# Expert weights copied three tiles ahead, and a dense item placed last: a change to the end of a vision tower kernel

## The chip, the cores and the metric

The kernel runs on one core of one Trainium2 chip. The metric is the device time of the whole kernel in microseconds, lower is better. The core has five engines that work side by side and wait for one another through semaphores: PE (TensorE, matmuls), DVE (VectorE), ACT (ScalarE), POOL (GpSimd, which here issues the indirect DMAs and a few powers) and SP (SyncE, which issues most other DMAs). Sixteen DMA engines move the data.

## The reference

The input is cut into patches and embedded (32 blocks of 512 tokens, 256 features each), run through one retention layer with an MLP, and then through a mixture of 8 experts of which each token uses two:

```python
logits = tokens @ router_w.T
probs = softmax(logits)
rw, re = top_k(probs, 2)
rw = rw / rw.sum(-1)
combine = zeros((N, E)).at[arange(N)[:, None], re].set(rw)
out = tokens
for e in range(8):
    h = gelu(tokens @ w1[e] + b1[e])
    y = h @ w2[e] + b2[e]
    out = out + combine[:, e:e+1] * y
```

Here `tokens` are the layer-normed outputs of the layer before, and the final result is those outputs plus `out`. All matmuls are in float32.

## The kernel before

A block of 512 tokens goes through embedding, retention, MLP and the router. Block 0 to 30 then *scatter* each token's row twice, once for each of its two experts, to a buffer in DRAM (`xbuf`) that has a region for each expert (`place`, eight indirect DMAs on GpSimd for a block). `take` looks how many *tiles* of 256 rows of one expert are full, and puts them into the list of tiles. A tile is worked through in stages, all driven by `expert_step`: `load` fetches its rows and its expert's weights, `turn` makes xT of the rows, `enter` multiplies by the first matrix, `leave` by the second, and adds the 256 results to `out` with two scatter-adds.

```python
    def expert_step():
        n = at["enter"]
        advance("load", n + AHEAD)       # AHEAD = 4
        advance("turn", n + 2)
        advance("fetch", n + 3)
        advance("enter", n + 1)
        advance("leave", n)
```

`advance(what, upto)` runs the stage `what` for all tiles before number `upto` that have not had it. PE, DVE, ACT and SP execute their instructions in the order in which this program emits them; the order on POOL is chosen by a scheduler.

Most tiles get their weights by a DMA in `load`. For the last 22 tiles (4 that are taken with block 29's choice, 18 with block 30's) all eight experts' weights are loaded once into SBUF, into `bank`, and VectorE copies the right one into the tile's buffer `w`:

```python
    def load_bank():
        ...
        for e in range(E):
            nc.scalar.dma_start(out=bank[0][:, e, :], in_=wex[ts(e, P), :])
            ...

        def fetch(self):                              # class Tile
            if self.block.i >= NS - 2:
                e = nc.vector.value_load(self.table[:, 2, t : t + 1], ...)
                nc.vector.tensor_copy(self.w.unsqueeze(1), bank[0][:, bass.ds(e, 1), :])
```

As the expert's number is only known at run time, such a copy waits for the whole bank. The end of `leave` scatters the sums; two pairs of scatter-adds may hit the same row, so a pair waits for the pair before it:

```python
            y = four.tile([P, 2, D], F32, name="y")
            nc.vector.tensor_tensor(y, ps, ..., ALU.add)               # L765
            for c in range(2):
                nc.vector.tensor_scalar(y[:, c, :], ...)               # L767
            before = added[-2:] + [self.block.stored]
            for c in range(2):
                add = nc.gpsimd.indirect_dma_start(out=out, ..., in_=y[:, c, :],
                                                   compute_op=ALU.add) # L771
                unordered("sums", add, before)
                added.append(add)
```

The last block (31) is not scattered. Its tokens go through all eight experts as *dense items* (`Expert(e, last)`), which stand in the same list as the tiles: an `enter` of eight matmuls (L803), a `leave` of sixteen (L820), and a sum into `h` on VectorE, weighted by the token's share. The last one stores `h`.

The stretch behind the main loop, where everything changed lies (NS is 31):

```python
        last, mid, old = blocks[NS], blocks[NS - 1], blocks[NS - 2]
        ...                                   # bank loads are issued in between
        old.choose()
        expert_step()
        next(weights)
        mid.mlp_out(0)
        next(weights)
        take(NS - 1, old, old.place())
        expert_step()
        mid.mlp_out(1)
        last.retention(0)
        mid.features3()
        mid.rows()
        last.retention(1)
        for t in range(TT):
            mid.logits(t)
        mid.choose()
        expert_step()
        writes = mid.place()
        last.residual()
        expert_step()
        expert_step()
        expert_step()
        mid.pads(writes)
        take(NS, mid, writes)

        last.features2()
        for m in range(KH):
            last.mlp_in(m)
        expert_step()
        last.mlp_out(0)
        expert_step()
        last.mlp_out(1)

        rest = tiles[at["load"] :]
        del tiles[at["load"] :]
        for e in range(E):
            tiles.extend(rest[len(rest) * e // E : len(rest) * (e + 1) // E])
            tiles.append(Expert(e, last))
        expert_step()
        expert_step()
        last.features3()
        ...                                   # logits of the last block
        last.choose()
        last.combine()
        while at["leave"] < len(tiles):
            expert_step()
```

Of the kernel before, what the change touches and what calls it, by code (L numbers as in the profile page):

```python
# [30 lines left out]
def vit_tower_kernel(  # L31
# [20 lines left out]
    E = rw.shape[1]  # L52
# [35 lines left out]
    def load_x(i):  # L88
        xb = xpool.tile([P, XW], F32, name="xb")
        nc.sync.dma_start(out=xb, in_=x[i // NBLK, i % NBLK])  # L90
        return xb
# [91 lines left out]
    def fold(w, g, b, to):  # L183

        n, M = w.shape[1], w.shape[3] // P
        ps = p_sm.tile([P, n * M], F32, name="sm")
        for i in range(n):
            for m in range(M):
                for k in range(KD):
                    nc.tensor.matmul(  # L190
                        ps[:, i * M + m : i * M + m + 1],
                        lhsT=w[:, i, k, ts(m, P)],
                        rhs=vec[:, b + k : b + k + 1],
                        start=k == 0,
                        stop=k == KD - 1,
                    )
        nc.vector.tensor_tensor(vec[:, to : to + n * M], vec[:, to : to + n * M], ps, ALU.add)
        for k in range(KD):
            nc.scalar.mul(w[:, :, k, :], w[:, :, k, :], vec[:, g + k : g + k + 1])
# [477 lines left out]
    def load_bank():  # L677

        early.close()
        late = ctx.enter_context(tc.tile_pool(name="late", bufs=1, side="right"))  # L680
        bank.append(late.tile([P, E, NW], F32, name="bank"))
        for e in range(E):
            nc.scalar.dma_start(out=bank[0][:, e, :], in_=wex[ts(e, P), :])
            loaded.append(e)
            yield

    AHEAD = 4
    tiles = []
# [155 lines left out]
    def advance(what, upto):  # L844
        while at[what] < min(upto, len(tiles)):
            getattr(tiles[at[what]], what)()
            at[what] += 1

    def expert_step():

        n = at["enter"]
        advance("load", n + AHEAD)
        advance("turn", n + 2)
        advance("fetch", n + 3)
        advance("enter", n + 1)
        advance("leave", n)

# [6 lines left out]
    def slot(known):  # L864

        if len(tiles) - at["enter"] > LEFT and at["enter"] + 2 <= known:
            expert_step()
# [7 lines left out]
    with tc.manual_schedule(engines=MANUAL):  # L875
        xs[1] = load_x(1)
        blocks[0].differences(xs.pop(0))
        for i in range(NS):
            new = blocks[i]
            known = len(tiles)  # L880
            mid = blocks[i - 1] if i >= 1 else None
            old = blocks[i - 2] if i >= 2 else None
            embed = new.embed()
            next(embed)
            if at["enter"] == 0:
                advance("turn", 2)
            if mid:
                mid.features2()
            if old:
                old.rows()  # L890
                old.turn3()
            next(embed)
            next(embed, None)
            slot(known)
            if old:
                old.join3()
            if i == 0:
                fold(wqkv_sb, G1, B1, BQ)
            for m in range(KH):
                if mid:  # L900
                    mid.mlp_in(m)
                if m == 1 and i:
                    new.split1()
                if m == TT - 1:
                    slot(known)
                if m == KH - 3:
                    new.features1()
            if old:
                for t in range(TT):
                    old.logits(t)  # L910
            blocks[i + 1].differences(xs.pop(i + 1))
            for m in range(KD):
                new.retention(m)
                if old and m == 0:
                    old.choose()
            if old:
                take(old.i + 1, old, old.place())
            if i + 2 < NB:
                xs[i + 2] = load_x(i + 2)
            slot(known)  # L920
            if mid:
                mid.mlp_out(0)
            new.residual()
            slot(known)
            if at["enter"] == 0:

                advance("load", 2)
            if i == 0:
                fold(w1_sb.unsqueeze(1), G2, B2, MB1)
            else:  # L930
                new.split2()
            if mid:
                mid.mlp_out(1)

        last, mid, old = blocks[NS], blocks[NS - 1], blocks[NS - 2]
        embed = last.embed()
        next(embed)
        mid.features2()
        old.rows()
        old.turn3()  # L940
        next(embed)
        next(embed, None)
        expert_step()
        weights = load_bank()
        old.join3()
        for m in range(KH):
            mid.mlp_in(m)
            if m in (1, 2, 4, 5, 7):
                next(weights)
            if m == 1:  # L950
                last.split1()
            if m == TT - 1:
                expert_step()
            if m == KH - 3:
                last.features1()
        for t in range(TT):
            old.logits(t)
# [4 lines that stand above are left out]
        mid.mlp_out(0)  # L962
        next(weights)
        take(NS - 1, old, old.place())
        expert_step()
        mid.mlp_out(1)
        last.retention(0)
        mid.features3()
# [22 lines that stand above are left out]
        rest = tiles[at["load"] :]  # L991
        del tiles[at["load"] :]
        for e in range(E):
            tiles.extend(rest[len(rest) * e // E : len(rest) * (e + 1) // E])
            tiles.append(Expert(e, last))
        expert_step()
        expert_step()
        last.features3()
        for t in range(TT):
            last.logits(t)  # L1000
# [4 lines that stand above are left out]
# [82 lines left out]
```

## Time and profile before

| what | value |
|---|---|
| time, median of three | 2275.05 us (2271.82 to 2275.25) |
| span of the profiled execution | 2277.5 us |
| PE busy | 2191.8 us, 96% |
| VectorE busy | 1490.3 us, 65% |
| GpSimd busy | 863.2 us, 38% |
| ScalarE busy | 784.9 us, 34% |
| scatter-adds to `out` (L771) | 262, 1655 ns each on GpSimd |
| copies of expert weights (L721) | 22, 0.83 us each |

A row of a timeline gives the start, the duration, the engine, the source line, the operation with the tile that it writes and those that it reads, and how many instructions were merged; the square bracket at the end says how long the engine was idle before it and which instruction released it. The releaser is inferred: an instruction that waits for several things is put down to the one that came last by the profile, and where the engine named had long been done it was another, often a DMA. The row of the page that shows PE's busy share in 40 slices of the span (56.9 us each) has it at nine tenths or more from the second slice on, except in the 37th (2050 to 2107 us) and in the last.

### The profile page before, as it was taken

Reading aid. Unit: us, or ns where it says so; the run is one execution under the profiler, and the core shown is the slowest. Engines: PE = TensorE matmul, PEld = TensorE weight load, DVE = VectorE, ACT = ScalarE, POOL = GpSimd, SP = SyncE. Lnnn points to the kernel's source line nnn. Section 1 sums busy time; section 2 is a strip of 40 time slices with the busy share of each in tenths; the row PEclk is TensorE's granted clock in tenths of the full one; section 3 lists DMA queues with packets and bytes.
Section 4 is the critical chain, followed back from the end, with each engine's and each line's share of the span. In section 5 each row is a group of like instructions: output and inputs, shape, how many; then the busy total and the mean of one; then the engine's idle time right before and its main releaser. Section 6 shows DMA issues by size and latency. Waiting matters only on the chain.

```text
span 2277.5 us, 28306 instructions
## 1 busy us (share of the span) xinstructions
PE 2191.8 (96%) x8652; PEld 1574.0 (69%) x8652; DVE 1490.3 (65%) x4427; ACT 784.9 (34%) x1213; POOL 863.2 (38%) x822
## 2 busy tenths in 40 slices
PE   3999999999999999999999999999999999997997
PEld 2666667777776677777667777676677777675775
DVE  6567666666666667666766666666667666757464
ACT  1222243333334333333343333334333333332332
POOL 0012224444443344443334444443444443335344
PEclk9999999999999999999999999999999999998999
DMA  5133357656656675566667656656665565595653
GB/s 150 28 94 82 102 128 158 136 128 135 143 129 131 150 158 118 130 140 138 136 131 159 132 130 134 143 128 132 152 152 123 131 140 137 117 180 111 120 68 46
DMA packets 461671, 289.14 MB, mean 127 GB/s; under 512 B 377936, under 2 KB 432336, under 8 KB 457424
## 3 DMA queue, kind: packets, MB, share of 16 engines
q1 hardware_dynamic: 410464, 214.44, 40.1%
q0 software_dynamic: 49632, 67.39, 16.9%
q10 hardware_dynamic: 1424, 5.52, 0.9%
q8 instruction: 68, 1.11, 0.2%
q14 instruction: 83, 0.68, 0.1%
HBM read 116.81 MB, written 88.39 MB: 90 GB/s over the span
## 4 chain that ended last, share of the span: by engine, by line
PE 51%; DVE 24%; POOL 11%; issue 7%; DMA 6%; ACT 0%; POOLq 0%; DVEq 0%; SPq 0%; ACTq 0%
PE mm L284 24%; PE tm L328 9%; POOL xbuf L576 8%; PE mm L734 5%; PE tm L751 5%; DMA out<-y,xg 4%; DVE ks L382 3%; DVE ret L392 3%; POOL out L771 2%; PE sm L493 2%; DVE kv L374 2%; DVE zz L238 2%; PE tm L442 2%; DVE h L417 1%; DVE h L416 1%
## 5 line engine op out<-in xcount | busy, mean ns | idle before, releaser
L771 POOL DMA_INDIRECT out<-y,xg x262 | 433.7, 1655 | 550.0 <-DVE y L767 302.4
L442 PE MATMUL tm<-w_sb,aT 128*128 128x256 f32 x2048 | 453.3, 379 | 1.7 <-DVE taken L671 1.1
L284 PE MATMUL mm<-hT,w_sb 128*128 128x512 f32 x1024 | 449.9, 593 | 1.6 <-ACT hT L278 1.1
L442 PEld LDWEIGHTS tm<-w_sb,aT 128*128 128x128 f32 x2048 | 388.6, 190 | 55.6 <-DVE taken L671 1.4
L284 PEld LDWEIGHTS mm<-hT,w_sb 128*128 128x128 f32 x1024 | 194.1, 190 | 223.0 <-issue 212.4
L284 PE MATMUL mm<-hT,wqkv_sb 128*128 128x512 f32 x768 | 342.9, 603 | 3.7 <-DVE hT L278 3.7
L576 POOL DMA_INDIRECT xbuf<-row,to x248 | 244.2, 985 | 257.2 <-DVE full L635 169.8
L742 ACT ACTIVATE ge<-mm,w 128x256 f32<-128x256 f32 x262 | 109.3, 469 | 522.0 <-issue 503.1
L284 PEld LDWEIGHTS mm<-hT,wqkv_sb 128*128 128x128 f32 x768 | 145.7, 193 | 175.8 <-issue 166.0
L734 PE MATMUL mm<-xT,w 128*128 128x256 f32 x1048 | 253.3, 385 | 9.7 <-DVE tile_share L760 9.1
L751 PE MATMUL tm<-w,ge 128*128 128x256 f32 x1048 | 248.8, 380 | 0.0
L434 ACT ACTIVATE aT<-mm,vec 128x512 f32<-128x512 f32 x256 | 171.3, 685 | 219.2 <-PE mm L284 218.2
L328 PE MATMUL tm<-weff,xd 128*128 128x256 f32 x1024 | 230.6, 384 | 16.8 <-DVE y L765 8.6
L328 PEld LDWEIGHTS tm<-weff,xd 128*128 128x128 f32 x1024 | 193.3, 191 | 53.2 <-DVE y L765 19.1
L734 PEld LDWEIGHTS mm<-xT,w 128*128 128x128 f32 x1048 | 196.2, 192 | 47.3 <-issue 23.2
L751 PEld LDWEIGHTS tm<-w,ge 128*128 128x128 f32 x1048 | 200.3, 191 | 31.1 <-issue 3.8
L727 ACT COPY xT<-xh 128x512 uint16<-128x512 uint16 x262 | 181.3, 761 | 39.7 <-DMA xh<-xbuf 32.4
L264 ACT COPY planes<-zz 128x1024 uint16<-128x1024 uint16 x122 | 121.5, 1043 | 206.0 <-DVE zz L238 206.0
L229 POOL TENSOR_SCALAR rstd<-mv 128x4 f32<-128x4 f32 x93 | 37.2, 400 | 328.2 <-DVE mv L210 326.1
L317 PE MATMUL tm<-wsum,xb 128*128 128x256 f32 x512 | 120.2, 389 | 25.8 <-ACT wsum L121 25.8
L238 DVE TENSOR_SCALAR zz<-z,mv,rstd 128x256 f32<-128x256 f32 x128 | 44.4, 410 | 137.7 <-POOL rstd L234 137.7
L533 POOL TENSOR_TENSOR ex<-euler,second 128x4 f32<-128x4 f32 x32 | 34.8, 1089 | 262.0 <-DVE second L525 262.0
(147 smaller groups left out, 2343.8 us busy)
## 6 DMA issues: line engine op xcount, KB each, us to landing
w<-in_wex SPq DMA_DIRECT2D x109, 641.5 KB
xb<-in_x SPq DMA_DIRECT2D x32, 1040.0 KB
out<-h SPq DMA_DIRECT2D x31, 512.0 KB
bank<-in_wex ACTq DMA_DIRECT2D x8, 641.5 KB
out<-y,xg POOLq DMA_INDIRECT x262
xbuf<-row,to POOLq DMA_INDIRECT x248
xh<-xbuf SPq DMA_TRANSPOSE x131
xg<-xbuf SPq DMA_DIRECT2D x131, 4.0 KB
```

Source lines behind the costliest of these rows:

```text
L264: nc.scalar.copy(planes[:, :, i * D : (i + 1) * D], half)
L284: nc.tensor.matmul(ps, lhsT=w[:, k, ts(m, P)], rhs=rhs[:, k, :], start=k == 0, stop=k == KD - 1)
L317: nc.tensor.matmul(ps[:, u, :], lhsT=od[:, j, ts(u, P)], rhs=wsum[:, j, :], start=j == 0, stop=j == J - 1)
L328: nc.tensor.matmul(ps[:, i, :], lhsT=xd[:, i, j, ts(u, P)], rhs=weff[:, i * J + j, :], start=j == 0, stop=j == J - 1,)
L434: nc.scalar.activation(self.aT[:, m, :], ps, AF.Relu, bias=vec[:, MB1 + m : MB1 + m + 1])
L442: nc.tensor.matmul(ps[:, i, :], lhsT=self.aT[:, k, ts(u * 2 + i, P)], rhs=w2_sb[:, k, :], start=k == 0, stop=k == KH - 1,)
L576: write = nc.gpsimd.indirect_dma_start(out=xbuf, out_offset=bass.IndirectOffsetOnAxis(ap=to[:, c, t : t + 1], axis=0), in_=self.row[:, t, ...
L727: nc.scalar.copy(halves[:, :, :, 1 - i], self.xh[:, i * KD : (i + 1) * KD, :])
L734: nc.tensor.matmul(ps[:, m, :], lhsT=self.w[:, k * D + m * P : k * D + (m + 1) * P], rhs=self.xT[:, k, :], start=k == 0, stop=k == KD - 1,)
L742: nc.scalar.activation(self.ge[:, m, :], ps[:, m, :], AF.Gelu, bias=self.w[:, 5 * D + m : 5 * D + m + 1])
L751: nc.tensor.matmul(ps[:, c, :], lhsT=self.ge[:, k, ts(c, P)], rhs=w[:, (2 + k) * D : (3 + k) * D], start=k == 0, stop=k == KD - 1,)
L771: add = nc.gpsimd.indirect_dma_start(out=out, out_offset=bass.IndirectOffsetOnAxis(ap=self.xg[:, c, NUMBER - D : NUMBER - D + 1], axis=0), ...
```

## The change

There are two edits, both behind the main loop. The first moves the copies of weights: a tile's copy is made as soon as its buffer is allotted in `load`, three tiles ahead of the one that enters and not two, and in the step behind block 29's `take` no copy is made at all, so that VectorE reaches no copy before it has worked through block 30's choice of experts. The three copies that have come due by then are made in the next step. It is meant to keep VectorE from standing still for the bank in front of work that others wait for, and PE from waiting for a copy. The second spreads the remaining tiles over the first seven dense items instead of over all eight, so that two dense items close the list and the last tile's sums are added while the last dense items still run.

```diff
-    def expert_step():
+    def expert_step(fetch=True):
 
         n = at["enter"]
         advance("load", n + AHEAD)
         advance("turn", n + 2)
-        advance("fetch", n + 3)
+        if fetch:
+            advance("fetch", n + AHEAD)
         advance("enter", n + 1)
         advance("leave", n)
 ...
         take(NS - 1, old, old.place())
-        expert_step()
+        expert_step(fetch=False)
         mid.mlp_out(1)
 ...
         for e in range(E):
-            tiles.extend(rest[len(rest) * e // E : len(rest) * (e + 1) // E])
+            tiles.extend(rest[len(rest) * e // (E - 1) : len(rest) * (e + 1) // (E - 1)])
             tiles.append(Expert(e, last))
```

In the built kernels the instructions of SP and their order are the same before and after, and so are those of POOL; PE, DVE and ACT have the same instructions in another order.

## The prediction, made before the changed kernel ran

> **What bounds the kernel now.** I read the page first: PE busy 96% of the span, so only what happens between matmuls can be gained. Every edit lies behind the main loop, so I then read the chain of waits from 2040 us on. I call the expert steps behind `take(NS - 1, ...)` A (where `fetch=False` is put), S1 (behind block 30's `choose`), S2, S3, S4 (behind `last.residual()`), S5 and S6 (in the last block's second half), S7 (behind `last.mlp_out(1)`'s matmuls, its y behind that item's VectorE work), S8 and so on.
>
> ```profile
> 2042.52 17.11 DMA bank<-in_wex
> 2059.75 0.83 DVE w L721
> ...
> 2067.86 2.33 PE mm L251 x8
> ...
> 2098.09 0.82 DVE w L721
> 2099.06 3.75 PE mm L734 x8
> ...
> 2262.50 4.18 DMA out<-y,xg
> 2266.80 0.71 issue
> 2267.51 1.54 POOL out L771
> ```
>
> Columns: start, duration, what. Twice a copy of an expert's weights (L721) stands ahead of PE on the path, the first behind the load of the bank. The end is not PE but GpSimd's scatter-adds. The timelines of PE, ScalarE and GpSimd give the sizes:
>
> ```profile
> 2054.51 5.31 PE L284 MATMUL mm<-hT,wqkv_sb 128*128 128x512 f32 x12
> 2067.86 2.33 PE L251 MATMUL mm<-ident,tok 128*128 128x128 f32 x8 [8.04 <-DVE rstd L223]
> ...
> 2084.16 1.99 PE L734 MATMUL mm<-xT,w 128*128 128x256 f32 x8 [0.64 <-ACT xT L727]
> ...
> 2099.06 3.75 PE L734 MATMUL mm<-xT,w 128*128 128x256 f32 x8 [7.73 <-DVE tile_share L760]
> ```
>
> ```profile
> 2082.72 1.39 ACT L727 COPY xT<-xh 128x512 uint16<-128x512 uint16 x2 [8.42 <-DMA xh<-xbuf]
> ```
>
> ```profile
> 2041.69 1.55 POOL L771 DMA_INDIRECT out<-y,xg  x1 [0.30 <-DVE row L521]
> 2061.42 1.60 POOL L771 DMA_INDIRECT out<-y,xg  x1 [17.04 <-DVE tile_share L763]
> ...
> 2150.99 1.54 POOL L771 DMA_INDIRECT out<-y,xg  x1 [11.97 <-DVE y L767]
> 2157.91 1.54 POOL L771 DMA_INDIRECT out<-y,xg  x1 [3.52 <-DMA out<-y,xg]
> ...
> 2254.18 1.54 POOL L771 DMA_INDIRECT out<-y,xg  x1 [3.05 <-DMA out<-y,xg]
> ...
> 2267.51 1.54 POOL L771 DMA_INDIRECT out<-y,xg  x1 [3.31 <-DMA out<-y,xg]
> ```
>
> The reader should see four things. PE idles 8.04 us ahead of the transposes of block 30's tokens, and 7.73 us ahead of S4. S2 begins at 2084.16 as soon as ScalarE has copied xT, which in its turn waited for rows out of `xbuf`. GpSimd sits from 2043.2 to 2061.4 before one scatter-add. And from 2150.99 on GpSimd starts a pair of scatter-adds every 6.9 us until the end: (2267.51 - 2150.99) / 17 = 6.85, each pair starting when the pair before has landed.
>
> **What the Trainium skill says.** "TensorE: Matmul & The Clock Gate", section "What's actually happening": PE falls to half clock after an idle window of about 3.4 us and comes back after about as long of work. The trace agrees that an idle costs more than itself: S4's eight enter matmuls took 3.75 us against 1.73 in later steps and its leave matmuls 2.35 against 1.73, 2.64 us lost behind 7.73 of idle. "DMA: Bandwidth & Descriptors", section "Rules for kernel authors": an accumulating DMA reads and writes later, so one that touches the same bytes must wait for the earlier one's semaphore. The kernel does this (`before = added[-2:]`), and the 3.05 to 3.9 us of idle between pairs are this wait. "SBUF — State Buffer", section "Who interferes with whom": a VectorE copy in a 2-port mode locks GpSimd out. A copy of 1283 columns is 0.83 us here, so it can hold a scatter back by about that much; only the spread of my range uses it.
>
> **The change, part by part.**
>
> *1. No copy in step A.* VectorE ends `take` at 2052.8 and then stands 6.93 us for the bank (2052.8 to 2059.75) plus 0.83 for the copy. Without it A's y (1.62 us) ends at 2054.5, and the h addition of `mlp_out(1)`, whose PE work ends at 2054.6, starts there instead of at 2062.11: 7.5 us earlier. The same chain (h to first tok, 5.2 us to 2067.30) then lets PE begin at about 2060.4 instead of 2067.86; PE's own work ends at 2059.8, so the 8.04 us gap becomes 0.6. Kept warm, PE also saves about 1.3 us in the transposes (2.33 against 1.04 for eight) and 1.8 in the twelve matmuls of retention(1) (6.99 against 5.2). PE thus finishes the residual transposes at about 2073.5 instead of 2083.5, 10 us ahead.
>
> *2. But S2 needs xT.* It is made from rows that block 29 scatters with eight L576 instructions. GpSimd has them in its order behind the scatter-add at 2061.42. The profile puts that wait down to a VectorE instruction, but its y was finished at 2045.1. What it also needs is the landing of the pair at 2039.83 and 2041.69, and in half-microsecond windows of the DMA the software queue and the bank's queue both carry their last bytes at 2059.5; the scatter-add starts 1.9 us later. So the bank load, which the change doesn't move, holds GpSimd. Then: pair at 2061.42 and 2063.32, eight scatters to 2076.6, transposing read at 2078.28, ScalarE at 2082.72, PE at 2084.16. None of this has the removed copy in it, and the order of GpSimd, SyncE and ScalarE here is the same in both built kernels. S2 stays at 2084.16, and part 1's 10 us become a wait of about 10.7 us before S2. Gain up to S2: 0.
>
> *3. Three copies in S1, one in S2.* S1 used to copy one set of weights and now copies three: about 0.77 + 3 x 0.8 = 3.2 us on VectorE against 1.6. VectorE is some 9 us ahead there, so this lies beside PE's wait. `place`'s weights need GpSimd's `ex`, ready at about 2082 whatever happens, so z is added from 2082.7 instead of 2087.36 and zz is done at 2091 instead of 2095.8. In S4 the weights have then been in place since 2078, and the 7.73 us wait goes. What ends last for S4: its xT, at 2092.3 (ScalarE's L727 at 2090.91 + 1.38; SyncE's reads don't move), or PE itself. PE comes out of 10.7 us of idle cold, as S4 does now: S2 takes 3.75 + 2.35 = 6.1 us, to 2090.3; S3 3.46, to 2093.7; S4 3.46, to 2097.2. The transposes of `features2` begin there instead of at 2105.16: **8.0 us** gained. The two floors: if S2 ran warm, xT would set S4 (2092.3 + 3.46 = 2095.8: 9.4 us); if zz set it, 2091 + 0.4, so it doesn't bind.
>
> *4. From there to S7.* PE is busy without a gap from 2106.28 to 2141. SyncE's padding and the reads of new tiles hang on S4's y and move along; GpSimd's pairs of S2 to S4 can start at about 2099.4, 2106 and 2113 and have caught up by S6 (y at 2127.7). The 8.0 us arrive whole at the y of S7, 2150.99 - 8.0 = 2143.0. One copy earlier than needed also removes the 1.33 us of PE's wait at 2166.42, behind `combine`.
>
> *5. The last dense item behind the last tile.* It brings the last tile's y forward by one half of a dense item, 6.9 us (3.43 + 3.46). But in the tail each y already waits for GpSimd: the y done at 2176.7 goes out at 2186.19, the one of 2209.4 at 2220.72, the last one, of 2261.2, at 2267.51. Bringing y forward lengthens this queue and not its pace: 2 tiles and one dense item are 13.8 us of PE, two pairs are 13.7 of GpSimd. y has four buffers and the queue is under 14 us, so nothing blocks VectorE. Gain 0; the 1.3 us of part 4 falls in the same hole. PE and the last store end some 13 us before the span does.
>
> Sum: -8.0 us on the pair that opens the unbroken series, the series itself unchanged. 2275.05 - 8.0 = **2267.0 us**.
>
> **Rivals.** (a) *Both gaps are worth their size*: 8.04 + 7.73 and about 5 us of cold clock make 2255 to 2260. It needs GpSimd's wait at 2061.42 to be VectorE's, as the profile labels it. Against it stand the y of 2045.1 and the DMA's last bytes at 2059.5. (b) *The dense item helps too*, another 3 to 7 us on top of mine: 2260 to 2264. It needs scatter-adds that keep up with y near the end; the queue of 4.6 us at the last but one pair and 6.3 at the last speaks against it. (c) *The wait just moves*: longer copies or the cold start of S2 hold the residual, or the reads of tiles take over: 2271 to 2275. For it speaks that S2's start is fixed and only S4's wait is left to gain; against it that VectorE has 5 us of slack at zz. (d) *A full queue of y blocks VectorE and then PE*, and the end moves later by a few us: 2276 to 2280. The 7 us between y's age (under 14 us) and its buffers' life (3 x 6.85 us) speak against it.
>
> **Range and chances.** Part 3's cold clock is uncertain by 1.5 us, GpSimd's spacing by 0.1 us x 17, and the three times of before spread by 3.4 us. Together with some weight for (a), (b) and (c) I take 2261.5 to 2271.5. All of these are under 2% (45 us): faster 0.01, within 0.98, slower 0.01.
>
> **What would show it.** Right: PE's gap before L251 is under 1 us; a gap of 9 to 12 us, released by xT, stands before S2 at about 2084; GpSimd's wait until 2061.4 is still there; S4 has no wait for VectorE; the pairs of the tail are 6.7 to 6.9 us apart, and the last two instructions on PE end over 10 us before the span. Wrong: if GpSimd's first pair comes much before 2061, part 2 falls and (a) holds. If the tail's spacing shrinks below 6.6 us or has gaps that wait for y, part 5 falls.

## The result, and the profile after

The changed kernel takes 2264.8 us (median of 4, 2261.87 to 2266.85) against 2273.4 us of the kernel before on the same chip: a ratio of 0.9961, with a 95% interval of 0.9944 to 0.9978, or 8.6 us less. The prediction was 2267.0, 8.0 less. The size is right. The way to it was not the one foretold, as the profile after shows at once. First the chain of waits (start, duration, what), at the two places shown before:

```profile
2057.81 0.70 DVE h L449
...
2063.59 1.21 PE mm L251 x4
...
2248.49 0.70 DVE zz L828
...
2250.12 4.10 DMA out<-y,xg
2254.34 0.71 issue
2255.05 1.54 POOL out L771
```

No copy and no bank load stands ahead of block 30's `h` any more, and the end is still GpSimd's pair of scatter-adds. PE's timeline after, from the second half of block 30's MLP on:

```profile
2050.70 7.07 PE L442 MATMUL tm<-w_sb,aT 128*128 128x256 f32 x32
2057.61 5.31 PE L284 MATMUL mm<-hT,wqkv_sb 128*128 128x512 f32 x12
2063.59 1.64 PE L251 MATMUL mm<-ident,tok 128*128 128x128 f32 x8 [0.67 <-DVE tok L238]
...
2077.62 1.96 PE L734 MATMUL mm<-xT,w 128*128 128x256 f32 x8 [0.22 <-DVE w L721]
2080.73 1.97 PE L751 MATMUL tm<-w,ge 128*128 128x256 f32 x8 [1.15 <-DVE y L765]
...
2091.24 1.73 PE L251 MATMUL mm<-ident,zz 128*128 128x128 f32 x8 [1.26 <-DVE zz L238]
```

The two gaps of 8.04 and 7.73 us are gone. So is the gap of 10.7 us that the prediction put before S2: S2 enters at 2077.62 with a wait of 0.22. GpSimd's timeline says why:

```profile
2037.02 1.55 POOL L771 DMA_INDIRECT out<-y,xg  x1 [0.30 <-issue]
...
2052.28 1.60 POOL L771 DMA_INDIRECT out<-y,xg  x1 [6.18 <-DVE full L629]
...
2139.07 1.76 POOL L771 DMA_INDIRECT out<-y,xg  x1 [9.67 <-DVE y L767]
...
2146.39 1.54 POOL L771 DMA_INDIRECT out<-y,xg  x1 [3.70 <-DMA out<-y,xg]
...
2248.27 1.54 POOL L771 DMA_INDIRECT out<-y,xg  x1 [3.04 <-DVE zz L828]
...
2255.05 1.54 POOL L771 DMA_INDIRECT out<-y,xg  x1 [3.39 <-DMA out<-y,xg]
```

The scatter-add behind block 29's choice starts 1.6 us behind the second half of block 30's MLP (2052.28 - 2050.70). In the profile of before it was 13.8 us (2061.42 - 2047.61). The tail is as foretold: from 2139.07 seventeen intervals to the last pair, (2255.05 - 2139.07) / 17 = 6.82 us against 6.85, and PE is done at 2248.5, over 16 us before the span ends.

The two programs first differ at step A's copy, which came up on VectorE 5.2 us behind the start of that L442 in before (2052.8 - 2047.61). In after the scatter-add starts ahead of this moment, and the second of the pair that it waits for was issued 13.7 us ahead of the L442 (2050.70 - 2037.02). So there are three theories:

1. *Fixed landing* (the prediction's step 2): the bank load always holds GpSimd as long as in the profile of before.
2. *Changing landing*: how the DMA traffic during the bank load falls out differs between executions, of either kernel; the profile of before shows a late one, that of after an early one.
3. *The change itself* freed GpSimd earlier.

### The profile page after: what moved, and what is told of

It is laid out like the page before. It is cut to its first block, busy times and chain, and to the rows that moved or that the text cites. A ratio compares the mean times of both kernels' runs of the same rounds, so it can differ in the third digit from the quotient of the medians.

```text
span 2265.0 us, 28306 instructions
## 1 busy us (share of the span) xinstructions
PE 2188.5 (97%) x8652; PEld 1570.3 (69%) x8652; DVE 1490.8 (66%) x4427; ACT 785.5 (35%) x1213; POOL 862.9 (38%) x822
## 4 chain that ended last, share of the span: by engine, by line
PE 55%; DVE 23%; POOL 9%; issue 6%; DMA 5%; SPq 1%; ACT 1%; DVEq 0%; POOLq 0%; ACTq 0%
PE mm L284 25%; PE tm L328 9%; POOL xbuf L576 7%; PE tm L751 6%; PE mm L734 6%; DMA out<-y,xg 4%; PE tm L442 3%; DVE ks L382 3%; PE sm L493 2%; DVE ret L392 2%; DVE zz L238 2%; POOL out L771 2%; DVE kv L374 2%; DVE h L417 2%; DVE h L416 2%
## 5 line engine op out<-in xcount | busy, mean ns | idle before, releaser
L442 PE MATMUL tm<-w_sb,aT 128*128 128x256 f32 x2048 | 453.1, 379 | 1.7 <-DVE h L449 1.7
L284 PE MATMUL mm<-hT,w_sb 128*128 128x512 f32 x1024 | 450.2, 593 | 2.1 <-ACT hT L278 1.1
L442 PEld LDWEIGHTS tm<-w_sb,aT 128*128 128x128 f32 x2048 | 388.6, 190 | 55.4 <-DVE h L449 2.1
L284 PEld LDWEIGHTS mm<-hT,w_sb 128*128 128x128 f32 x1024 | 194.1, 190 | 223.8 <-issue 212.1
L284 PE MATMUL mm<-hT,wqkv_sb 128*128 128x512 f32 x768 | 342.4, 602 | 4.7 <-DVE hT L278 4.5
L284 PEld LDWEIGHTS mm<-hT,wqkv_sb 128*128 128x128 f32 x768 | 145.4, 193 | 176.7 <-issue 167.3
L734 PEld LDWEIGHTS mm<-xT,w 128*128 128x128 f32 x1048 | 194.6, 190 | 37.7 <-issue 13.8
```

Source lines behind the costliest of these rows:

```text
L284: nc.tensor.matmul(ps, lhsT=w[:, k, ts(m, P)], rhs=rhs[:, k, :], start=k == 0, stop=k == KD - 1)
L442: nc.tensor.matmul(ps[:, i, :], lhsT=self.aT[:, k, ts(u * 2 + i, P)], rhs=w2_sb[:, k, :], start=k == 0, stop=k == KH - 1,)
L734: nc.tensor.matmul(ps[:, m, :], lhsT=self.w[:, k * D + m * P : k * D + (m + 1) * P], rhs=self.xT[:, k, :], start=k == 0, stop=k == KD - 1,)
```

## The experiments

All times stand in one table, each against the kernel before on the same chip. The kernel before was timed anew for each group of kernels; its medians lie between 2272.3 and 2274.0 us, so medians of different groups are compared only to a us or two.

| kernel | median us | ratio to before, 95% interval |
|---|---|---|
| after | 2264.8 | 0.9961 (0.9944 to 0.9978) |
| copies_only | 2264.1 | 0.9955 (0.9939 to 0.9971) |
| dense_only | 2275.5 | 1.0004 (0.9990 to 1.0018) |
| skip_only | 2271.3 | 0.9980 (0.9971 to 0.9990) |
| ahead_only | 2265.4 | 0.9958 (0.9949 to 0.9968) |
| before_small_bank | 2270.9 | 0.9983 (0.9974 to 0.9992) |
| after_small_bank | 2260.7 | 0.9939 (0.9919 to 0.9959) |
| early_steps_2 | 2261.3 | 0.9943 (0.9925 to 0.9960) |
| early_steps_3 | 2261.8 | 0.9948 (0.9929 to 0.9966) |
| early_steps_3_spread | 2266.4 | 0.9961 (0.9947 to 0.9975) |
| early_steps_3_late_share | 2257.1 | 0.9934 (0.9920 to 0.9947) |

**Both kernels profiled again** (before_again, after_again; no edit but a comment).

> The kernel before, profiled a second time. Theory 1 (the prediction's step 2): the bank load ends about 7 us behind the take of block 29 on VectorE and holds GpSimd's scatter-add until 2 us later, always. Then this profile repeats the first: 17 us of wait on GpSimd, 8 us of PE idle before block 30's token transposes, 7.7 us before S4. Theory 2 (the traffic on the DMA queues during the bank load falls out differently from execution to execution): the bank's last bytes and the scatter-add move by 3 us or more against PE's work, and with them VectorE's wait for the bank and the span. Theory 3 (the change itself freed GpSimd earlier): as theory 1 for this kernel.

> The changed kernel, profiled a second time. Theory 1: GpSimd's scatter-add behind the bank load starts some 15 us behind the start of block 30's mlp_out(1) on PE and S2 waits about 10 us for xT. Theory 2: it may come anywhere from 0 to 14 us behind it, and S2's wait for xT with it. Theory 3: it comes early again, within 1 us of the first profile of this kernel (about 1.6 us behind that start), with no wait of S2 for xT.

PE's and GpSimd's timelines of the kernel before in its second profile:

```profile
2049.66 7.07 PE L442 MATMUL tm<-w_sb,aT 128*128 128x256 f32 x32
...
2063.20 1.64 PE L251 MATMUL mm<-ident,tok 128*128 128x128 f32 x8 [1.31 <-DVE tok L238]
...
2092.35 3.75 PE L734 MATMUL mm<-xT,w 128*128 128x256 f32 x8 [8.44 <-DVE tile_share L760]
```

```profile
2040.75 1.55 POOL L771 DMA_INDIRECT out<-y,xg  x1 [0.30 <-DVE top L516]
...
2052.73 1.60 POOL L771 DMA_INDIRECT out<-y,xg  x1 [9.34 <-DVE past L658]
```

The same program, but GpSimd starts 3.1 us behind PE's L442 and not 13.8, the idle before block 30's token transposes is 1.31 us and not 8.04, and VectorE's idle before the copy in A is 1.21 us and not 6.93. VectorE's copy in A, in the first profile, in the second, and in before_small_bank below (where the line is L722):

```profile
2059.75 0.83 DVE L721 COPY w<-bank 128x1283 f32 x1 [6.93 <-DMA bank<-in_wex]
```

```profile
2054.99 0.83 DVE L721 COPY w<-bank 128x1283 f32 x1 [1.21 <-ACT xT L727]
```

```profile
2052.48 0.84 DVE L722 COPY w<-bank 128x1283 f32 x1 [1.20 <-issue]
```

With a quarter of the bank the idle is as long as in the second profile, so in the second profile VectorE did not wait for the bank at all. Only the wait of S4 for its weights is the same in both, 8.44 against 7.73, with the same cold clock behind it (3.75 us for eight matmuls). The changed kernel's second profile is an early one again (1.7 us). Theory 1 falls and theory 2 holds. Theory 3 falls too: the kernel before shows an early landing, and skip_only below, which has the edit in A, a late one. A sign of this stood in the record beforehand: the profile's span of 2277.5 us is longer than each of the three timed runs of the kernel before (2271.82 to 2275.25).

To compare executions I count from the start of that L442 in each profile (us), to the scatter-add and to the last block's MLP (the L284 x32), with PE's waits before S2 and S4. The last four kernels, described below, have the whole first edit, and their own changes lie behind this stretch:

| profile | scatter-add starts | wait before S2 | wait before S4 | last MLP starts |
|---|---|---|---|---|
| before | +13.8 | 0.64 | 7.73 | +58.7 |
| before_again | +3.1 | none | 8.44 | +49.6 |
| dense_only | +0.2 | none | 8.40 | +51.8 |
| skip_only | +14.3 | 9.81 | 0.92 | +51.4 |
| ahead_only | +0.7 | none | none | +42.9 |
| copies_only | +0.5 | 0.56 | none | +42.1 |
| after | +1.6 | 0.22 | none | +42.5 |
| after_again | +1.7 | 0.22 | none | +42.4 |
| before_small_bank | -6.8 | none | 8.41 | +49.6 |
| after_small_bank | -5.9 | none | none | +41.9 |
| early_steps_2 | +8.2 | 2.83 | none | +43.2 |
| early_steps_3 | +0.9 | 0.62 | none | +42.3 |
| early_steps_3_spread | +1.6 | 0.21 | none | +42.0 |
| early_steps_3_late_share | +12.0 | 7.47 | none | +49.4 |

Early against early (before_again and after_again), the stretch loses 49.6 - 42.4 = 7.2 us; with dense_only and after it is 9.3, as twelve matmuls (L284) in dense_only took 6.94 us against 5.42. Both profiles of the changed kernel are early ones. Late against late, skip_only loses 58.7 - 51.4 = 7.3 us, but makes no copy earlier; early_steps_3_late_share, with the whole first edit, loses 58.7 - 49.4 = 9.3, though its scatter-add is 1.8 us less late. PE in this kernel:

```profile
2082.13 3.78 PE L734 MATMUL mm<-xT,w 128*128 128x256 f32 x8 [7.47 <-ACT xT L727]
...
2091.54 1.89 PE L734 MATMUL mm<-xT,w 128*128 128x256 f32 x8
```

This is what the prediction had drawn: a long wait for xT before S2, and none before S4.

The timed runs suggest how often the kernel before pays for a late landing. Of its 61 runs beside skip_only, 17 took over 2278 us; of skip_only's 22 none took over 2275.8, and of before_small_bank's 20 none over 2273.7. The late profile of before took 2279.3 us, the early before_again 2272.9, and the late skip_only 2269.2. That the 17 are late executions is not shown, as they were not profiled.

**The two edits apart.**

```diff
 # copies_only: the changed kernel, with
-            tiles.extend(rest[len(rest) * e // (E - 1) : len(rest) * (e + 1) // (E - 1)])
+            tiles.extend(rest[len(rest) * e // E : len(rest) * (e + 1) // E])
 # dense_only: the kernel before, with the opposite of that
```

> The first edit alone (no copy in step A, copies three tiles ahead), the dense items as before. If the tail is bound by the scatter-adds, as the prediction's step 5 has it, this gives the whole gain: 2264 to 2267 against 2273.4 before, and the last scatter-add still stands on the path. If the dense item's place is worth its 6.9 us, this gives only 2 us: 2270 to 2273.

> The second edit alone (the last dense item behind the last tile), copies as before. Step 5: no gain, 2272 to 2275, the pairs of scatter-adds 6.7 to 6.9 us apart to the end, and PE done over 10 us before the span ends. The rival (y's readiness sets the end): 2266 to 2269.

The copies alone give the whole gain (0.9955), the dense item alone nothing that shows (1.0004, the interval from 0.9990 to 1.0018); its 2275.5 us lie just above the range of 2272 to 2275. The last pairs of dense_only on GpSimd:

```profile
2251.54 1.54 POOL L771 DMA_INDIRECT out<-y,xg  x1 [3.07 <-DMA out<-y,xg]
...
2257.89 1.54 POOL L771 DMA_INDIRECT out<-y,xg  x1 [2.96 <-DMA out<-y,xg]
...
2264.32 1.54 POOL L771 DMA_INDIRECT out<-y,xg  x1 [3.04 <-DVE h L834]
```

These last pairs stand 6.4 us apart and wait for one another (over all seventeen intervals it is (2264.32 - 2145.94) / 17 = 6.96, a little over the 6.7 to 6.9 expected), while the last matmuls ended at 2264.2. The last tile's y is earlier now, and its scatter-add is not. The expected "over 10 us" between PE's end and the span's came out at 10.1 (2274.3 - 2264.2).

**The two halves of the first edit.**

```diff
 # skip_only: the kernel before, with expert_step(fetch=False) in step A
 # ahead_only: the kernel before, with
-        advance("fetch", n + 3)
+        advance("fetch", n + AHEAD)
```

> Only the missing copy in step A (copies still two ahead, dense items as before). Two theories of where the gain of about 9 us comes from. Theory S4: in most executions VectorE waits for the bank hardly at all in step A, and the gain is the 8.4 us wait of S4 for its weights, whose copy is still in S2 behind the residual here: then 2271 to 2275, and the wait of about 8 us on PE ahead of S4 stays. Theory A: the copy in step A was the obstacle: then 2264 to 2268.

> Only the copies three tiles ahead (a copy is made in step A too, now two of them, dense items as before). Theory S4: most of the gain, 2264 to 2268, with no wait of S4 for VectorE; PE's gap ahead of block 30's token transposes is about 2 us longer than without copies in A, as two copies and their loads of the number lie before it. Theory A: two copies behind the bank in A cost more than one: 2273 to 2277.

ahead_only is worth 0.9958, nearly the whole. skip_only's 0.9980 is small but clear of 1, and fits a gain in late executions only. So the gain is mostly S4's: a copy made a step earlier stands in front of the residual on VectorE, and S4 no longer waits for it. PE in ahead_only:

```profile
2046.26 7.07 PE L442 MATMUL tm<-w_sb,aT 128*128 128x256 f32 x32
...
2060.99 2.29 PE L251 MATMUL mm<-ident,tok 128*128 128x128 f32 x8 [2.51 <-DVE tok L238]
...
2087.23 1.73 PE L251 MATMUL mm<-ident,zz 128*128 128x128 f32 x8 [0.77 <-DVE zz L238]
```

The two copies in A lengthen the gap before the transposes to 2.51 us (0.67 after), and no wait of S4 is left. The profile of skip_only fell on a late execution, and shows the prediction's wait for xT. Its PE, ScalarE and GpSimd:

```profile
2047.52 7.07 PE L442 MATMUL tm<-w_sb,aT 128*128 128x256 f32 x32
...
2083.82 3.78 PE L734 MATMUL mm<-xT,w 128*128 128x256 f32 x8 [9.81 <-DVE st L209]
...
2094.11 1.97 PE L734 MATMUL mm<-xT,w 128*128 128x256 f32 x8 [0.92 <-DVE tile_share L760]
```

```profile
2082.38 1.38 ACT L727 COPY xT<-xh 128x512 uint16<-128x512 uint16 x2 [17.39 <-DMA xh<-xbuf]
```

```profile
2040.89 1.55 POOL L771 DMA_INDIRECT out<-y,xg  x1 [0.30 <-DVE row L521]
...
2061.82 1.93 POOL L771 DMA_INDIRECT out<-y,xg  x1 [18.25 <-DVE tok L238]
```

GpSimd is free at 2061.82, xT is made at 2082.38 to 2083.76, and PE waits 9.81 us and starts S2 cold (3.78 us) at 2083.82. The label "DVE st" at PE's wait is beside the point: the last thing S2 needs is xT, which ends 0.06 us earlier. The wait of about 8 us before S4, which theory S4 expected to stay, is 0.92 here: while PE waited for xT, VectorE got through the residual and the copy behind it, which ended at 2093.96. An early execution of skip_only was not profiled.

**A small bank.** Is it the bank load that holds GpSimd?

```diff
-        bank.append(late.tile([P, E, NW], F32, name="bank"))
+        bank.append(late.tile([P, 2, NW], F32, name="bank"))
         for e in range(E):
-            nc.scalar.dma_start(out=bank[0][:, e, :], in_=wex[ts(e, P), :])
+            if e < 2:
+                nc.scalar.dma_start(out=bank[0][:, e, :], in_=wex[ts(e, P), :])
 # and the expert's number is cut to 0 or 1 wherever the bank is read
```

> The kernel before with a bank of two experts instead of eight, loaded by two DMAs of 641.5 KB instead of eight (it leaves the other six experts' weights out, and uses the first two in their place). If the bank load is what holds GpSimd's scatter-adds and VectorE there, then the scatter-add behind block 29's choice starts within 6 us of the one before it, VectorE's copy in A doesn't wait, and S4's wait of about 8 us for its weights stays as it is: 2270 to 2273. If something else holds them, the scatter-add still stands 9 us or more.

> The changed kernel with the same small bank (six experts' weights left out). Theory S4: the distance to the kernel before with the small bank is that of the full kernels, 8 to 10 us, as it has nothing to do with the bank: 2261 to 2264. Theory A (the bank in front of VectorE): the distance falls to under 3 us.

It is. GpSimd in after_small_bank:

```profile
2035.10 1.74 POOL L772 DMA_INDIRECT out<-y,xg  x1 [0.30 <-issue]
...
2042.21 1.61 POOL L772 DMA_INDIRECT out<-y,xg  x1 [1.99 <-DVE y L768]
```

The scatter-add now waits for its y alone, and starts 5.9 us ahead of the L442 in place of 0.2 to 14.3 us behind it. PE in before_small_bank still waits before S4:

```profile
2089.75 3.75 PE L735 MATMUL mm<-xT,w 128*128 128x256 f32 x8 [8.41 <-DVE tile_share L761]
```

The distance between the two kernels is 10.2 us (2270.9 to 2260.7), no less than with the full bank and a little over the 8 to 10 expected. So the gain does not need the bank in front of VectorE. Leaving out six loads is worth about 3 us to the kernel before (0.9983); for the changed one the medians differ by 4, but the intervals overlap.

**Is the series of scatter-adds the end?** If so, filling GpSimd's idle time ahead of it must help. The 9.67 us of idle before 2139.07 come from VectorE, which works the last block's norm before S7's y.

```diff
         expert_step()
         last.mlp_out(0)
         expert_step()
+        expert_step()      # early_steps_2: two of these, early_steps_3: three
+        expert_step()
         last.mlp_out(1)
 # early_steps_3_spread: three, on copies_only
```

> The changed kernel with two more expert steps in front of the last block's second MLP half, so that two pairs of scatter-adds fill GpSimd's gap of some 13 us there. If the unbroken series of pairs sets the end (step 5), two of its 17 intervals of 6.85 us are taken out and its start moves by two steps of 3.46 us on PE: 13.7 - 6.9 = 6.8 us, less what the reads of tiles hold PE up: 2258 to 2262. If PE's end sets it: no gain, 2264 to 2267.

> The same with three more steps. If the series sets the end: up to 10 us below the changed kernel, but PE and the last store then end at the same time as the series, so 2255 to 2260.

> The same three steps, with the last dense item where it was before the change, ahead of nothing: a tile's sums close the list. If the place of the dense item is without effect only because the series of scatter-adds lags behind, it must count once the series starts earlier: this is 2 to 5 us slower than with two dense items last. If its place never counts: the same within 1.5 us.

early_steps_2 and early_steps_3 come out about 3 us below the changed kernel, at 2261.3 and 2261.8, with intervals that overlap its own. This is at the edge of the range for two steps and outside that for three. early_steps_3_spread is 4.6 us slower than early_steps_3 (2266.4 against 2261.8), as expected if the place of the dense item counts once the series starts earlier. The two intervals overlap, so the times only suggest it. The trace agrees, as GpSimd in early_steps_3_spread waits for y near the end and no longer for the pair before:

```profile
2240.60 1.54 POOL L771 DMA_INDIRECT out<-y,xg  x1 [4.94 <-DVE y L767]
...
2249.24 1.54 POOL L771 DMA_INDIRECT out<-y,xg  x1 [5.25 <-DVE y L767]
```

The chain at the end of early_steps_3:

```profile
2247.92 6.94 PE tm L820 x32
...
2254.88 0.70 DVE zz L828
...
2255.61 0.48 DVE h L834
2256.09 0.40 DVEq L1087
```

No scatter-add is left in it: PE sets the end. What kept PE from ending at 2248.5, as in after, stands in its own timeline and VectorE's:

```profile
2166.26 3.75 PE L734 MATMUL mm<-xT,w 128*128 128x256 f32 x8 [7.04 <-DVE tile_share L760]
```

```profile
2163.47 0.17 DVE L538 TENSOR_SCALAR share<-ex 128x4 f32<-128x4 f32 x1 [11.93 <-POOL ex L533]
```

VectorE waits 11.93 us for GpSimd's `ex`, which stands in GpSimd's order behind the scatter-adds, and the copy of the next tile's weights stands behind that. A new wait had taken the place of the old one. The last kernel puts `combine` where its result is first needed:

```diff
         last.choose()
+        expert_step()
+        expert_step()
         last.combine()
```

> Three more steps ahead of the last MLP half, and the last block's combine (which waits for GpSimd's ex behind the queue of scatter-adds) two expert steps later, just ahead of its first use. If that wait on VectorE is what held PE for 7.0 us in front of a tile, with about 2.6 us of cold clock behind it, the gap falls under 1 us, the series of scatter-adds sets the end again, and the time is 1.5 to 4 us below the version with combine at its old place: 2257.5 to 2260.5. If PE is held by y itself (its buffers or its PSUM), the gap stays and the time is the same, 2261 to 2263.

2257.1 us, 0.9934 (0.9920 to 0.9947), a little below the range. PE at that place now:

```profile
2162.71 3.60 PE L803 MATMUL mm<-tokT,bank 128*128 128x512 f32 x8
2166.14 1.89 PE L751 MATMUL tm<-w,ge 128*128 128x256 f32 x8
2167.87 1.89 PE L734 MATMUL mm<-xT,w 128*128 128x256 f32 x8
2169.60 3.62 PE L820 MATMUL tm<-bank,kv 128*128 128x256 f32 x16
```

There is no bracket, so no idle. This kernel beats both, by 15 us the one before and by 6 to 8 the changed one (0.9934 against 0.9961, 2257.1 against 2264.8). Its interval touches that of the changed kernel only between 0.9944 and 0.9947. Against early_steps_3 it is 4.7 us by the medians, but these intervals overlap; what the trace shows is that the gap is gone. Its profile fell on a late execution, the longest of its five, and the end there is PE's and the store's, not the scatter-adds', which was not expected.

## Why the prediction was right in size, and which steps failed

*Step 1* (the bank in front of VectorE in A, 7.5 us): true of the profile it was read from, and not of every execution. The idle before A's copy was 6.93 us there, 1.21 us in before_again, and 1.20 with the small bank, where no wait for it is left. I took one execution for all.

*Step 2* (GpSimd held by the bank load, S2 fixed by xT): the mechanism was right, and its fixed time was wrong. That the label on GpSimd's 17 us was false, and that the bank load holds the scatter-adds, the small bank shows; that S2 then waits for xT, skip_only and early_steps_3_late_share show (9.81 and 7.47 us against 10.7 foretold). But the sentence "S2 stays at 2084.16" failed: in both profiles of after, GpSimd started 1.6 and 1.7 us behind PE's L442, and S2 waited 0.22 us for a copy. The prediction had named a pair much before 2061 as the sign that this step is wrong. It came at 2052.28, and yet rival (a), which it said would then hold, did not come.

*Step 3* (S4's wait goes: 8.0 us) carries the gain. The wait is gone in every profile with the copies three tiles ahead, early or late, and the stretch is 7.2 us shorter in early executions. Two terms of the step were off for the early kind. PE has no cold start in S2, since there is no long idle before it. In its place the copies bind: with the loads of their numbers they took 4.1 us on VectorE (2075.49 to 2079.62) and not 3.2, and "this lies beside PE's wait" and "zz doesn't bind" failed by 0.22 + 1.15 + 1.26 us of PE waiting for a copy, for y and for zz. That the size came out right is therefore in part luck: the 8.0 us were worked out for a late execution, and in the early ones the gain is made of other terms. There 8.44 us of wait and 2.2 us of cold clock in S4 go (5.66 us from its start to the next transposes in before_again, against 3.46), and 3.2 us within S2 to S4 come (13.62 us in after, against six times 1.73), with 0.22 before S2: 7.2.

*Step 4* (the gain arrives whole, and 1.33 us more behind `combine`): PE waited 0.88 and 0.26 us for the xT of the first new tile in the two profiles of after, so not quite without a gap. The wait behind `combine` is gone; no run shows what it is worth alone.

*Step 5* (the dense item: 0): right, by dense_only. Its reason, that the series of scatter-adds lags behind y, is supported by the waits in dense_only's trace and by the kernels with early steps. Rival (a) foretold 2255 to 2260 and rival (b) 2260 to 2264; after lies above both. Rival (c)'s moved wait was seen in the late executions of three other kernels (2.83, 7.47 and 9.81 us before S2), and there it didn't take the gain away. Rival (d) didn't show. That a copy on VectorE holds GpSimd back, which the prediction used for its range, no run here tests.

It stays open what makes an execution early or late. When the pair before was issued does not settle it: its first scatter-add stands 7.8 and 8.7 us ahead of the L442 in the late before and skip_only, but 11.7 and 13.8 in the late early_steps_3_late_share and early_steps_2, and 11.2 in the early before_again. I made no experiment on it.

## What to carry to other kernels

A wait for a DMA in one profile is one draw: profile the unchanged kernel a second time before a gap that a busy DMA queue sets is counted as a gain, and trust the gaps that repeat (here S4's 7.73, 8.44, 8.40 and 8.41 us in four profiles without the earlier copies). A copy that another engine will need should stand in the program ahead of the long serial work on its own engine, not behind it. Bringing work forward pays nothing where a serial series of transfers lags behind it anyway; start the series earlier first, and look for what has waited in its shadow.

## What the hardware showed that was not expected

The same scatter-adds, issued at nearly the same point of the program, released the next pair between 0.2 and 14.3 us behind the same matmul, over twelve profiled executions with the full bank. With a quarter of the bank it was 5.9 and 6.8 us ahead of it.

Half speed on PE was seen again and again behind idle of 7 to 10 us (3.75 us for eight matmuls behind 7.04, 7.73 and 8.44 us, 3.78 behind 7.47 and 9.81, against 1.89 in the timelines of later steps). Below that, the length of the idle does not tell the speed: eight matmuls took 3.57 us behind 2.83 us (early_steps_2, S2), twelve took 6.94 soon behind 1.59 (dense_only) but 5.42 soon behind 1.31 (before_again), and in the kernel before eight took 3.14 at 2151.09, with no idle over 0.24 us just before them and a granted clock of 0.67 from 2151.1 to 2156.3. So the idle window of about 3.4 us that the prediction took over is no sure bound here.
